# Products of a row with itself: pieces, places and rows on a 256-byte grid, and another order of the last waits

## Chip, cores and metric

The kernel runs on one core of one Trainium2 chip. The metric is the device time of one execution in microseconds. It was run three times before the change, and the median counts.

## What is computed

```python
# r_inputs: float32 (4096, 256)
d = inputs.shape[1]
dot = jnp.einsum('bi,bj->bij', inputs, inputs)
iu, ju = jnp.triu_indices(d)
return dot[:, iu, ju]          # float32 (4096, 32896)
```

Each of 4096 rows of 256 numbers becomes 32896 numbers: all products of two of its elements, with the second index not below the first. The 256 runs of an output row, one for each first index i, have the lengths 256, 255, ... 1. The input has 4.19 MB and the output 538.97 MB.

## The kernel before

**Tiling.** Partition p of 128 holds 32 input rows, all of them in `xt`, which stays on the chip for the whole run. Two rows at a time (`REPEAT`) are worked on together, so one round has 512 numbers a partition. There are 16 rounds, two to a pass (`PASS` of 6 pieces is two rounds of `PIECES` = 3). A round's output row of 32896 columns is cut into three pieces by `even_borders`, in steps of `UNIT` = 32 columns: 10944, 10976 and 10976 columns wide.

**Buffers.** There are two output places `o0` and `o1` (`PLACES`), each with two rows of `slot` = 10976 columns a partition; piece p goes to place p % 2. A place holds 87808 bytes a partition, its rows lie 43904 bytes apart. In the order of allocation the tiles are `xt`, `xv` (a copy of the round's input for VectorE and GpSimd), `xa` (the same for ScalarE, used at the start alone), and then the places; `xp`, in PSUM, is a further copy that VectorE reads. In the built program `xt` starts at byte 16512 of a partition, `xv` at 49280, `xa` at 51360, `o0` at 53408 and `o1` at 141216.

**Engines.** Each piece's runs are divided over engines. VectorE (L220) multiplies the row `xv` by a number from `xp` that is repeated along the run, with two neighbouring runs in one instruction where that is possible; GpSimd (L272) does the same from `xv` alone. The division in the loop gives GpSimd about 19.4 us of work by a cost formula and VectorE the rest. The first two pieces (`AHEAD`) come before the loop: for them ScalarE (L244) works beside VectorE in GpSimd's place, and the first piece leaves in five parts (`FIRST`) so that stores start early. ScalarE first copies its input to `xa` (L239).

**Order.** SyncE issues every DMA: three loads of the input (L327), which take 128 x 512, 3584 and 4096 numbers, and then one store for each piece or part (L298). A store waits for `v_done` and for `a_done` or `g_done`, and its landing adds 16 to `free0` or `free1`. Before it writes a place, VectorE waits for that place's landing and tells GpSimd by `go`. A pass of the loop (L310) makes pieces 2 to 5 of one pass and then 0 and 1 of the next. `take` (L164) is the helper that waits for a semaphore and takes the count off.

**The end.** After the loop SyncE passes six waits by `take`: `free0`, `free1`, then `x_read`, then the three `loaded`. Then all engines meet and the program ends.

One store row, 43904 bytes of one partition, is one DMA packet; each of the 16 DMA engines has 16 of the 256 rows of a store.

Of the kernel before, what the change touches and what calls it, by code (L numbers as in the profile page):

```python
# [8 lines left out]
F32 = mybir.dt.float32  # L9
AF = mybir.ActivationFunctionType  # L10
ALU = mybir.AluOpType

P = 128
UNIT = 32
REPEAT = 2
PIECES = 3
PLACES = 2
SETS = 2
PASS = 6
# [7 lines left out]
def even_borders(lo: int, hi: int, pieces: int) -> list[int]:  # L27
    units = (hi - lo) // UNIT
    return [lo + units * c // pieces * UNIT for c in range(pieces)] + [hi]

# [83 lines left out]
def kernel(  # L114
# [15 lines left out]
    nc = tc.nc  # L130
    n, d = x.shape
    width = out.shape[1]
    each, groups = REPEAT * d, n // (P * REPEAT)
    rounds = PASS // PIECES
    passes = groups // rounds
    assert n % (P * REPEAT) == 0 and width == d * (d + 1) // 2 and width % UNIT == 0
    assert PASS % PLACES == 0 and AHEAD == PLACES and PASS % PIECES == groups % rounds == 0
    borders = even_borders(0, width, PIECES)
    spans = list(zip(borders, borders[1:]))
    slot = max(b - a for a, b in spans)  # L140
# [2 lines left out]
    x_out = out.rearrange("(p h q r) c -> h q p r c", p=P, q=rounds, r=REPEAT)  # L143

    pool = ctx.enter_context(tc.tile_pool(name="all", bufs=1))
    xt = pool.tile([P, passes, rounds * each], F32, name="x")

    xv = pool.tile([P, each + 1], F32, name="xv")
    xa = pool.tile([P, each], F32, name="xa")

    xp = ctx.enter_context(tc.tile_pool(name="psum", bufs=1, space=bass.MemoryType.PSUM)).tile([P, each], F32, name="xp")
    places = [pool.tile([P, REPEAT, slot], F32, name=f"o{k}") for k in range(PLACES)]
    ctx.enter_context(tc.tile_critical())  # L153

    def semaphore(name: str):
        return ctx.enter_context(nc.semaphore(name))

    free = [semaphore(f"free{k}") for k in range(PLACES)]
    head, v_done, a_done, go = (semaphore(s) for s in ("head", "v_done", "a_done", "go"))
# [3 lines left out]
    def take(engine, sem, value: int):  # L163
        engine.wait_ge(sem, value).then_inc(sem, -value)  # L164

    v_own, a_own, g_own = (semaphore(s) for s in ("v_own", "a_own", "g_own"))
    g_done, x_read = semaphore("g_done"), semaphore("x_read")

    def x_of(h, q: int) -> bass.AP:
        return xt[:, bass.ds(h, 1), q * each : (q + 1) * each].rearrange("p o d -> p (o d)")  # L170

    def blocks(p: int, ahead: bool):

        lo, hi = spans[p % PIECES]
        cuts = [lo, *(FIRST if ahead and p == 0 else []), hi]
        for a, b in zip(cuts, cuts[1:]):
            block = runs(d, a, b)
            if ahead:
                k = split(block)
                yield a - lo, b - lo, block[:k], block[k:], lo  # L180
            else:
                k = next(k for k in range(len(block)) if gpsimd_time(block[k:]) <= BUDGET * 1e3)
                yield a - lo, b - lo, block[k:], block[:k], lo

    uses = PASS // PLACES

    def use(p: int) -> int:
        return (p - AHEAD) % PASS // PLACES + 1  # L190

    def vector(h, pieces: range, ahead: bool, done: int = 0) -> int:
        for p in pieces:
            place = places[p % PLACES]
            if p % PIECES == 0:
                if not ahead:
                    take(nc.vector, x_read, 1)
                for to in (xv[:, :each], xp):
                    ins = nc.vector.tensor_copy(to, x_of(h, p // PIECES))  # L199
                    if done:  # L200
# [35 lines left out]

    def scalar(pieces: range):

        nc.scalar.activation(xa, x_of(0, 0), AF.Copy).then_inc(a_own, 1)  # L239
        take(nc.scalar, a_own, 1)  # L240
        for p in pieces:
            for _, _, block, _, lo in blocks(p, True):
                todo = [
                    nc.scalar.activation(  # L244
                        places[p][:, r, at - lo : at - lo + length],
                        xa[:, r * d + j : r * d + j + length],
                        AF.Copy,
                        scale=xa[:, r * d + i : r * d + i + 1],
                    )
                    for i, j, at, length in block  # L250
                    for r in range(REPEAT)
                ]
                if todo:
                    todo[-1].then_inc(a_done, 1)
                else:
                    nc.scalar.sem_inc(a_done, 1)
# [45 lines left out]
    def all_pieces(engine, pieces_of):  # L302
        done = pieces_of(0, range(AHEAD), True)
        if engine is nc.vector:
            nc.vector.sem_inc(v_own, -done)
        if engine is not nc.sync:
            for sem in loaded[1:]:
                engine.wait_ge(sem, 16)
        kind = engine.engine
        with nc.Fori(  # L310
            0,
            passes,
            engines=OrderedEngineSet([kind]),
            head_slot={kind: 0} if engine is not nc.sync else {},
        ) as h:
            done = pieces_of(h, range(AHEAD, PASS), False)
            with engine.If(h < passes - 1):
                nxt = nc.s_assert_within(h + 1, 0, passes - 1)
                if engine is nc.vector:
                    nc.vector.sem_inc(v_own, -vector(nxt, range(AHEAD), False, done))  # L320
                else:
                    pieces_of(nxt, range(AHEAD), False)
        if engine is nc.vector:
            nc.vector.sem_inc(v_own, -done)
# [7 lines left out]
    take(nc.tensor, head, 16 * (len(FIRST) + 1))  # L332
    nc.tensor.sem_inc(free[0], 16)
    scalar(range(AHEAD))
    for engine, pieces_of in ((nc.vector, vector), (nc.gpsimd, gpsimd), (nc.sync, sync)):
        all_pieces(engine, pieces_of)
    for k in range(PLACES):
        take(nc.sync, free[k], 16 * uses)
    take(nc.sync, x_read, 1)
    for sem in loaded:  # L340
        take(nc.sync, sem, 16)


# [25 lines left out]
```

## Time and profile before

| what | value |
|---|---|
| median of 3 runs | 1270.35 us (1270.26 to 1270.4) |
| the profiled execution, given by its span alone | 1268.8 us |
| DVE busy | 794.1 us, 63% |
| POOL busy | 767.8 us, 61% |
| ACT busy | 29.9 us, 2% |
| queue 1 of the DMA | 99.5% of 16 engines |
| store of 10976 columns | 10976 KB, x32, 32.1 us from issue to landing (median) |
| store of 10944 columns | 10944 KB, x15, 33.6 us |

The span runs from the first to the last instruction of the program in the profile; the timed runs are 1.55 us above it, and the profile gives no other time for its execution. DVE is VectorE, ACT ScalarE, POOL GpSimd, SP SyncE; a small q behind a name stands for the engine's instruction queue. The time from issue to landing counts the time behind other stores in the same queue.

### The profile page before, as it was taken

What the parts mean: (1) busy time and instruction counts of PE and PEld (TensorE: products, weight loads), DVE (VectorE), ACT (ScalarE), POOL (GpSimd) and SP (SyncE); (2) the same over time, 40 slices, a digit from 0 to 9 for tenths busy, and PEclk for the clock granted to TensorE, in tenths of its full rate; (3) what the DMA queues carried; (4) which work ended last, traced back from release to release, by engine and by line L of the source; (5) the groups of instructions that cost most, each with busy time, mean ns of one, the idle gap of its engine ahead of it and who ended that gap; (6) DMA issues with size and microseconds to landing.
All of it is one profiled execution on the core that took longest, in us unless ns stands there. A gap on an engine that the chain in (4) does not pass through costs nothing. (4 is left out here: it accounts for less than half of the span.)

```text
span 1268.8 us, 3000 instructions
## 1 busy us (share of the span) xinstructions
DVE 794.1 (63%) x1197; ACT 29.9 (2%) x80; POOL 767.8 (61%) x1032
## 2 busy tenths in 40 slices
DVE  8756856567466674766648665486655866468560
ACT  9000000000000000000000000000000000000000
POOL 0467674676647765577556765567656675576750
DMA  9999999999999999999999999999999999999997
GB/s 379 438 437 425 439 431 433 434 428 433 431 435 429 437 426 438 426 437 424 439 425 439 427 436 429 435 430 433 430 433 428 435 421 441 421 442 421 438 425 336
DMA packets 14583, 543.22 MB, mean 428 GB/s; under 512 B 880, under 2 KB 880, under 8 KB 1520
## 3 DMA queue, kind: packets, MB, share of 16 engines
q1 hardware_dynamic: 14576, 543.17, 99.5%
q14 instruction: 7, 0.06, 0.0%
HBM read 4.19 MB, written 538.97 MB: 428 GB/s over the span
## 5 line engine op out<-in xcount | busy, mean ns | idle before, releaser
L272 POOL TENSOR_TENSOR o<-xv 128x292 f32<-128x292 f32 (+60 forms) x1028 | 767.6, 787 | 461.8 <-DVEq L207 322.1
L220 DVE TENSOR_TENSOR o<-xv,xp 128x512 f32<-128x512 f32 (+61 forms) x1164 | 776.1, 746 | 429.4 <-DMA out_dram<-o 303.8
L244 ACT ACTIVATE o<-xa 128x253 f32<-128x253 f32 (+38 forms) x78 | 27.9, 454 | 0.2 <-ACTq L164 0.2
L199 DVE COPY xv<-x 128x512 f32 (+1 forms) x16 | 6.8, 427 | 10.0 <-DVEq L164 7.2
L199 DVE COPY xp<-x 128x512 f32 (+1 forms) x16 | 11.1, 695 | 0.6
L239 ACT ACT_TABLE_LOAD x1 | 1.3, 1283 | 0.9 <-SPq L153 0.9
L328 DVE MEMSET xv<- 128x1 f32 x1 | 0.1, 59 | 1.0 <-SPq L153 1.0
L239 ACT ACTIVATE xa<-x 128x512 f32<-128x512 f32 x1 | 0.6, 631 | 1.7 <-DMA x<-in_r_inputs_dram 1.7
L356 POOL MEMSET const-float32-0.0<- 128x1 f32 x1 | 0.1, 98 | 0.2 <-issue 0.2
L356 POOL MEMSET const-bfloat16-1.0<- 128x1 bf16 x1 | 0.1, 101 | 0.0
L356 POOL MEMSET const-uint8-127<- 128x1 uint8 x1 | 0.1, 101 | 0.0
L356 POOL MEMSET const-float32-1.0<- 128x1 f32 x1 | 0.1, 98 | 0.0
## 6 DMA issues: line engine op xcount, KB each, us to landing
out_dram<-o SPq DMA_DIRECT2D x32, 10976.0 KB, 32.1
out_dram<-o SPq DMA_DIRECT2D x15, 10944.0 KB, 33.6
out_dram<-o SPq DMA_DIRECT2D x1, 4544.0 KB, 19.4
out_dram<-o SPq DMA_DIRECT2D x1, 2816.0 KB, 15.1
x<-in_r_inputs_dram SPq DMA_DIRECT2D x1, 2048.0 KB, 12.4
out_dram<-o SPq DMA_DIRECT2D x1, 2048.0 KB, 12.6
x<-in_r_inputs_dram SPq DMA_DIRECT2D x1, 1792.0 KB, 7.1
out_dram<-o SPq DMA_DIRECT2D x1, 1024.0 KB, 9.7
```

The lines of the kernel that those rows point to most:

```text
L199: ins = nc.vector.tensor_copy(to, x_of(h, p // PIECES))
L220: ins = nc.vector.tensor_tensor(place[:, :, at : at + m * length], window(xv[:, j:], [[d, REPEAT], [1, m], [1, length]]), window(xp[:, i:] ...
L239: nc.scalar.activation(xa, x_of(0, 0), AF.Copy).then_inc(a_own, 1)
L244: nc.scalar.activation(places[p][:, r, at - lo : at - lo + length], xa[:, r * d + j : r * d + j + length], AF.Copy, scale=xa[:, r * d + i ...
L272: ins = nc.gpsimd.tensor_tensor(place[:, :, at : at + m * length], window(xv[:, j:], [[d, REPEAT], [1, m], [1, length]]), window(xv[:, i:] ...
L328: nc.vector.memset(xv[:, each:], 0.0)
L356: nc = _bacc.Bacc("TRN2", target_bir_lowering=False, num_devices=1)
```

## The change

`UNIT` becomes 64 columns, 256 bytes, and the borders of the pieces move to 0, 10944, 21888 and 32896; the pieces are 10944, 10944 and 11008 columns wide. A tile `edge` of 32 numbers, which nothing uses, comes first, then the places, then `xt` and `xv`. In the built program `o0` starts at byte 16640, `o1` at 104704, `xt` at 192768 and `xv` at 225536; all four are multiples of 256, and so is the distance of 44032 bytes between the rows of a place. ScalarE has no copy of its own: `xa` is now the first 512 numbers of `xt`, and the copy and its wait are gone. SyncE's last waits come in the order `x_read`, the three `loaded`, `free0`, `free1`.

```diff
-UNIT = 32
+UNIT = 64
 REPEAT = 2
 PIECES = 3
+EDGE = 32
 ...
     pool = ctx.enter_context(tc.tile_pool(name="all", bufs=1))
+    pool.tile([P, EDGE], F32, name="edge")
+    places = [pool.tile([P, REPEAT, slot], F32, name=f"o{k}") for k in range(PLACES)]
     xt = pool.tile([P, passes, rounds * each], F32, name="x")
-
     xv = pool.tile([P, each + 1], F32, name="xv")
-    xa = pool.tile([P, each], F32, name="xa")
 
     xp = ctx.enter_context(tc.tile_pool(name="psum", bufs=1, space=bass.MemoryType.PSUM)).tile([P, each], F32, name="xp")
-    places = [pool.tile([P, REPEAT, slot], F32, name=f"o{k}") for k in range(PLACES)]
 ...
-    v_own, a_own, g_own = (semaphore(s) for s in ("v_own", "a_own", "g_own"))
+    v_own, g_own = (semaphore(s) for s in ("v_own", "g_own"))
 ...
     def scalar(pieces: range):
 
-        nc.scalar.activation(xa, x_of(0, 0), AF.Copy).then_inc(a_own, 1)
-        take(nc.scalar, a_own, 1)
+        xa = xt[:, 0, :each]
 ...
-    for k in range(PLACES):
-        take(nc.sync, free[k], 16 * uses)
     take(nc.sync, x_read, 1)
     for sem in loaded:
         take(nc.sync, sem, 16)
+    for k in range(PLACES):
+        take(nc.sync, free[k], 16 * uses)
```

## The prediction

> **What bounds the kernel now.** I read the DMA rows of the page first, because the output is 539 MB and the engines are idle a third of the time.
>
> ```profile
> DVE 794.1 (63%) x1197; ACT 29.9 (2%) x80; POOL 767.8 (61%) x1032
> ...
> DMA  9999999999999999999999999999999999999997
> ...
> q1 hardware_dynamic: 14576, 543.17, 99.5%
> ...
> HBM read 4.19 MB, written 538.97 MB: 428 GB/s over the span
> ```
>
> No compute engine passes 63%, and the DMA row is full in every slice but the last. Queue 1, which carries the three loads and all stores, fills 99.5% of the span. The second view is the waits, to see whether the DMA waits for the engines or they for it.
>
> ```profile
> POOL o L272 <- DVEq L207: 322.1, 32, 43.1
> DVE o L220 <- DMA out_dram<-o: 303.8, 31, 12.3
> ...
> DVE o L220 <- DVEq L164: 119.2, 14, 12.4
> ```
>
> VectorE waits for stores to land and so to free a place (L164 is the waiting helper, and DVEq L207 the wait that releases GpSimd). The stores never wait long for VectorE. The third view, busy time in stretches, gives the pace of the stores.
>
> ```profile
> 66.00:92.00 26.00, 13.72 (x14) 0.00 (x0) 17.94 (x12) 1.00 1.00 434
> ...
> 470.00:548.00 78.00, 49.15 (x75) 0.00 (x0) 49.97 (x66) 1.00 1.00 432
> ...
> 1184.00:1210.00 26.00, 14.63 (x19) 0.00 (x0) 17.70 (x16) 1.00 1.00 431
> 1236.50:1262.40 25.90, 0.00 (x0) 0.00 (x0) 0.00 (x0) 1.00 0.96 414
> 1240.00:1266.80 26.80, 0.00 (x0) 0.00 (x0) 0.00 (x0) 1.00 0.80 346
> 1266.80:1268.80 2.00, 0.00 (x0) 0.00 (x0) 0.00 (x0) 1.00 0.00 0
> ```
>
> The columns are the length, the three engines, the clock, the DMA share and GB/s. The pace is 431 to 434 GB/s, whatever the engines do beside it. The last 2.0 us hold no transfer. From 1262.4 to 1266.8 only part of the DMA engines still works: the packet records show one engine that ends 4.3 us after the median of the others. That engine never runs dry, and it sets the end. The time is therefore: start of the stream, plus the packets of one DMA engine, plus the 2.0 us after them.
>
> [...]
>
> **The change, part by part.**
>
> *Addresses of the stores.* In the program built from the kernel before, places start at byte 160 past a multiple of 256, and with a row of 43904 bytes their second row starts at 32 past. [...] One packet is one row of one piece. A DMA engine carries 16 of the 256 rows of each of 47 whole pieces and of the 5 parts of the first: 832 packets. [...]
>
> Does the trace charge it? The packet records say no, in three ways. First, in the head the median store packet of 2048, 4096, 8192, 11264 and 18176 bytes took 84, 159, 309, 422 and 676 ns: a line of 36.7 ns a KB (1000 bytes) that leaves 8.8 ns at zero length. Records of one DMA engine overlap by 3.5 ns, so a packet really loses about 5.3 ns[...]. Second, the loads, whose source rows do start at multiples of 256, lie on the same line: 84 ns for 2048 bytes and 535 for 14336. Third, [...]in each head part nearly all packets have one and the same duration (309 from the 1st to the 75th percentile and beyond, at 8192 bytes). I take 0.5 ns a packet, 832 x 0.5 = 0.4 us[...].
>
> *Borders in the output.* Rows of the third piece started at 128 past a multiple of 256, those of the first at 0. Once the stream has settled, three pieces in a row took 26.03, 26.02 and 25.94 us (second, third, first; semaphore to semaphore). The first has 43776 bytes a row, not 43904; scaled by that it would be 26.02. So a border off the grid costs 0.00 to 0.01 us a piece, over the 32 second and third pieces at most 0.3 us. I take zero, as bytes in all are unchanged.
>
> [...]In the loop the median packet of 43904 bytes took 1627 ns and the mean is some 1630, where the line gives 1620.5. These 7 to 10 ns are not the offsets, which the head had too without them: the first whole pieces were at 1622, and they rise once the DMA engines drift apart. I price the change on them at zero, and keep plus or minus 3 ns for the range (2.5 us).
>
> *ScalarE's copy.* One ACTIVATE of 631 ns and its wait go, and ScalarE starts at about 3.9 us instead of 4.71.
>
> ```profile
> 3.88 0.63 ACT L239 ACTIVATE xa<-x 128x512 f32<-128x512 f32 x1 [1.69 <-DMA x<-in_r_inputs_dram]
> 4.71 27.95 ACT L244 ACTIVATE o<-xa 128x253 f32<-128x253 f32 x78 [0.20 <-ACTq L164]
> 5.08 32.03 DVE L220 TENSOR_TENSOR o<-xv,xp 128x512 f32<-128x512 f32 x45
> 6.59 31.10 SPq L298 DMA_DIRECT2D out_dram<-o  x6
> ```
>
> ScalarE ended at 32.7 us and VectorE at 37.1, and the issue at 37.3 followed VectorE. The first parts are covered twice: the loads held the queue until 14 us and each of the five parts was issued over 5 us before the queue came to it. Worth 0. If that cover were gone it would be worth 0.8 us at most.
>
> *Pieces of 10944, 10944, 11008 columns* (before 10944, 10976, 10976). The built program shortens one GpSimd and one VectorE instruction of the second piece by 64 elements and lengthens one VectorE instruction of the third by 64: 64 x 1.07 ns (from 1222 ns for 1024 elements and 1020 for 836) = 0.07 us, beside 19.92 us for that piece (last group of the chain). It is covered on the DMA engine that sets the end, which has 4.3 us of work left when the last store is issued; on the others only some 0.2 us is left by then, and they do not count. The last store is 32 KB longer, 0.08 us, but the bytes of a DMA engine are the same in all: 0.
>
> *SyncE's last waits.* The last packet ends at 1266.80, its semaphore rises at 1267.28, and SyncE then passes five waits, for place 1, x_read and three loads, at 1267.295, .362, .428, .496 and .562. After the change only that for place 1 stands behind the landing; the others had long been met. Four times 0.067 = **0.27 us** less, on the path, as everything after waits for SyncE.
>
> Sum: 0.27 + 0.4 = 0.7 us less. The span of 1268.8 becomes 1268.1; the median of the runs stands 1.55 above that span, and I take that distance to stay: 1270.35 - 0.7 = **1269.6**. [...]
>
> **The rivals.**
>
> [...]
>
> *Slower: rows in step.* All places, rows and borders now fall on the same phase of 256 bytes, and if the DMA engines get more into each other's way, packets lengthen. The place is the loop; the trace shows such growth, from 1622.7 ns mean for the second whole store to 1630 later. Another 4 ns is 832 x 4 = 3.3 us: 1273.0. It decides from 2.54 / 832 = 3.1 ns. Against it: each packet keeps its length and its DMA engine.
>
> *Engines become the bound.* If xv and the places at new addresses slowed VectorE, the third piece's 19.92 us would have to grow by 4.3 us (22%) before the latest DMA engine runs dry. Nothing speaks for it: the same instructions run on the same operands. Past that point every place that waits for this piece adds the excess.
>
> *The change does nothing but the tail:* 1270.1, inside the first case.
>
> **How the numbers follow.** A measurement of this kernel can tell about 0.2%, 2.54 us: faster is below 1267.8, slower above 1272.9. First case with the tail alone: 0.70. Offsets at full price or more: 0.21. Rows in step or slower engines: 0.09; of these about 0.02 stays below 1272.9. So faster 0.21, same 0.72, slower 0.07. The range runs from 1266.9[...] to 1271.2, which leaves out the slower case and the part of the faster one that adds the drift, and takes in a drift that worsens by 1 to 2 ns.
>
> **What would show it.** Right: a pace of 432 to 433 GB/s in the same stretches, median packets near 1622 ns (43776 bytes) and 1632 (44032), one wait of SyncE after the last landing and the end some 1.75 us after the last packet; ScalarE's first ACTIVATE at 3.9 and no earlier first landing. Wrong: packets on or below the head's line (1616 and 1625 ns) and 434 GB/s or more, which is the offsets; packets 4 ns longer, which is the rows in step; DMA slices under 9 inside the loop, which is the engines.

## The result, and the profile after

| | median | range | runs |
|---|---|---|---|
| before | 1270.36 us | 1270.23 to 1270.63 | 16 |
| after | 1267.88 us | 1267.78 to 1268.03 | 16 |

The ratio of after to before is 0.998, with a 95% interval of 0.9974 to 0.9987. The kernel is 2.48 us faster, 0.2%. The profiled span fell by 2.7 us, from 1268.8 to 1266.1.

These are the lines of the page of after that answer to those of before.

```profile
DVE 795.2 (63%) x1197; ACT 29.2 (2%) x79; POOL 766.1 (61%) x1032
...
DMA  9999999999999999999999999999999999999997
...
q1 hardware_dynamic: 14576, 543.17, 99.4%
...
HBM read 4.19 MB, written 538.97 MB: 429 GB/s over the span
```

Nothing changed its role: the DMA is full and the engines have time. The waits of after say the same; VectorE waits for places as long as it did (302.0 us now, 303.8 before).

```profile
POOL o L271 <- DVEq L207: 322.5, 32, 43.0
DVE o L220 <- DMA out_dram<-o: 302.0, 31, 12.3
```

Busy time in stretches of after (length, three engines, clock, DMA share, GB/s):

```profile
66.00:92.00 26.00, 13.72 (x14) 0.00 (x0) 17.93 (x12) 1.00 1.01 437
470.00:548.00 78.00, 49.36 (x75) 0.00 (x0) 49.98 (x67) 1.00 1.01 435
1184.00:1210.00 26.00, 14.63 (x19) 0.00 (x0) 17.59 (x16) 1.00 1.00 431
1236.50:1262.40 25.90, 0.00 (x0) 0.00 (x0) 0.00 (x0) 1.00 0.89 384
...
1260.50:1264.50 4.00, 0.00 (x0) 0.00 (x0) 0.00 (x0) 1.00 0.05 22
1264.50:1266.10 1.60, 0.00 (x0) 0.00 (x0) 0.00 (x0) 1.00 0.00 0
```

The pace in the middle rose from 432 to 435 GB/s, and yet the last row but one is what counts: over the last 4.0 us a share of 0.05 of 16 DMA engines moves data, which is about one of them. The stretch before the end shows the same in the kernel before:

```profile
1262.60:1266.80 4.20, 0.00 (x0) 0.00 (x0) 0.00 (x0) 1.00 0.05 21
```

So the other DMA engines became faster (median packet in the loop 1622 ns for 43776 bytes and 1627 for 43904 before, 1618 for 43776 and 1627 for 44032 after), and then wait at the places, which are free only when all 16 have landed, for the one that is late. It sets the time as before. The packet records do not name the DMA engines; the late one is followed by the last of a store's 16 semaphore packets, one from each DMA engine (880 packets under 512 bytes for 55 transfers). What it needs for a piece (from one such packet to the next, mean of the pieces of the loop) is the key to all that follows. The row lengths are in brackets.

| kernel | first piece, us | second | third |
|---|---|---|---|
| before | 25.95 (43776 B) | 26.24 (43904) | 26.06 (43904) |
| after | 25.93 (43776) | 26.11 (43776) | 26.07 (44032) |

The second piece lost 128 bytes a row and 0.13 us; the third gained 128 bytes a row and next to nothing. Each comes once in 16 rounds: 16 x 0.13 = 2.1 us, and the shorter end of the program gives 0.3 (experiment 6).

### The profile page after: what moved, and what is told of

Its sections match the earlier page's. It is cut to its first block, busy times and chain, and to the rows that moved or that the text cites. A ratio compares the mean times of both kernels' runs of the same rounds, so it can differ in the third digit from the quotient of the medians.

```text
span 1266.1 us, 2998 instructions
## 1 busy us (share of the span) xinstructions
DVE 795.2 (63%) x1197; ACT 29.2 (2%) x79; POOL 766.1 (61%) x1032
## 5 line engine op out<-in xcount | busy, mean ns | idle before, releaser
L220 DVE TENSOR_TENSOR o<-xv,xp 128x512 f32<-128x512 f32 (+61 forms) x1164 | 777.1, 748 | 426.3 <-DMA out_dram<-o 302.0
L243 ACT ACTIVATE o<-x 128x253 f32<-128x253 f32 (+38 forms) x78 | 28.0, 454 | 0.0
```

The lines of the kernel that those rows point to most:

```text
L220: ins = nc.vector.tensor_tensor(place[:, :, at : at + m * length], window(xv[:, j:], [[d, REPEAT], [1, m], [1, length]]), window(xp[:, i:] ...
L243: nc.scalar.activation(places[p][:, r, at - lo : at - lo + length], xa[:, r * d + j : r * d + j + length], AF.Copy, scale=xa[:, r * d + i ...
```

## The experiments

The times of the kernel before in these comparisons were 1270.38, 1270.38 and 1270.39 us.

**1. Borders back.** Only the borders in the output leave the grid again; the rows in the places stay on it.

```diff
-UNIT = 64
+UNIT = 32
-    slot = max(b - a for a, b in spans)
+    slot = -(-max(b - a for a, b in spans) // 64) * 64
```

Theory G has every packet cost the same extra whose source row and output row stand at different distances from the 256-byte grid; theory B has the borders in the output alone count.

> The changed kernel with the borders of the pieces back at 10944 and 21920 columns (steps of 32); places, rows and input stay on the 256-byte grid. [...] Theory G[...]: only the third piece's rows start at 128 past, a third of the packets lose what they lost before: 1268.6. Theory B (borders in the output are what counted): as before but for the tail, 1270.1, with the third piece's packets alone longer.

Measured: 1270.27 us (1270.13 to 1270.46), ratio to before 0.9999 [0.9991, 1.0008]. Nearly the whole gain is gone, so it came from the borders. The DMA engine that ends last needs 25.94, 26.24 and 26.06 us for the three pieces, which are the numbers of before; the longer piece is the second and not the third, as theory B had it. The page of this kernel shows the 2.4 us in the span, and its stretches a pace in the middle as high as that of after:

```profile
span 1268.5 us, 2998 instructions
```

```profile
470.00:548.00 78.00, 49.15 (x75) 0.00 (x0) 49.96 (x66) 1.00 1.01 435
```

In this run the packets of the other DMA engines hardly vary: the median in the loop is 1618 ns for 43776 bytes and 1622 for 43904, where before had 1622 and 1627. It brought no time.

**2 to 4. The places off the grid by 32, 128 and 224 bytes.** The borders stay on the grid.

```diff
-EDGE = 32
+EDGE = 40      # 64 and 88 in the other two
```

> The changed kernel with every tile 32 bytes further, so that all source rows start at 32 past a multiple of 256 and the output stays on the grid. [...] G: any offset costs the same, about as before less the tail: 1270.1. B: 1267.9.

> The same with 128 bytes. [...] G: 1270.1; if what counts is a grid of 64 bytes and not of 256, 1267.9. B: 1267.9.

> The same with 224 bytes. [...] G: 1270.1, also if the grid has 64 bytes. B: 1267.9.

Measured: 1267.66 (1267.48 to 1267.82), 1267.71 (1267.54 to 1267.93) and 1267.74 us (1267.56 to 1267.88), ratios 0.9979 [0.997, 0.9987] for each of the first two and 0.9979 [0.9971, 0.9987] for the third. 32, 128 and 224 bytes of distance cost the same: nothing that the time shows. The distance of the source rows from the grid does not set the time here, and theory G falls. The offsets are visible all the same. With each of the three distances the median packet in the loop is 1622 ns (43776 bytes) and 1632 (44032), where after has 1618 and 1627. Busy time in stretches of the kernel with 32 bytes:

```profile
470.00:548.00 78.00, 49.34 (x75) 0.00 (x0) 50.03 (x67) 1.00 1.00 431
...
1184.00:1210.00 26.00, 14.63 (x19) 0.00 (x0) 17.61 (x16) 1.00 1.00 431
...
1261.80:1264.30 2.50, 0.00 (x0) 0.00 (x0) 0.00 (x0) 1.00 0.04 18
```

The pace in the middle is back at 431 GB/s from 435, while the time is 0.2 us shorter than after. The last row tells why: the late DMA engine, which sets the end, is alone for some 2.5 us here and for 4.0 in after; it ends at 1264.3 in one and 1264.5 in the other. A faster mean pace was spent on waiting for it.

**5. Borders off by 32 bytes.** Both inner borders move by 8 columns.

```diff
-    borders = even_borders(0, width, PIECES)
+    borders = [0, 10952, 21896, width]
```

Theory W counts 256-byte blocks of the output: on the DMA engine that ends last, a row that starts or ends inside a block costs as much as one that fills it.

> The changed kernel with both inner borders 8 columns (32 bytes) further, at 10952 and 21896. Theory W[...]: a round's three rows of pieces touch 172 + 172 + 172 = 516 of them, against 514 in the changed kernel and 515 before. One more costs 9.4 ns a packet, x 16 packets x 16 rounds = 2.4 us, so two cost 4.8: 1272.7 us. [...] Rival, bytes alone: 1267.9.

Measured: 1272.72 us (1272.57 to 1272.9), ratio 1.0018 [1.0011, 1.0026], to the tenth what theory W said, and 4.8 us over after. On the DMA engine that ends last the first piece went from 25.93 to 26.07 us: 16 packets that are 32 bytes longer, 1.2 ns at the 36.7 ns for 1000 bytes of the head's packets, took 8.4 ns more each. The second, with rows of 43776 bytes as in after but across the grid, went from 26.11 to 26.27. The third, whose 44000 bytes touch 172 blocks like the 44032 of after, stayed within 0.02. The size of the block is not settled by this, and no record shows blocks as such; the count fits the times. With blocks of 128 bytes before and after would count the same (1028 a round), and they differ by 2.4 us; but blocks of 512 bytes fit as well as 256: an output row is 257 of them, so that successive rows start on and half a block off their grid, and the means of a round are 258.5 in after, 259 in before and 259.5 here, the same steps of 256 bytes. The page:

```profile
span 1271.2 us, 2996 instructions
```

**6. The tail alone,** on the kernel before.

```diff
-    for k in range(PLACES):
-        take(nc.sync, free[k], 16 * uses)
     take(nc.sync, x_read, 1)
     for sem in loaded:
         take(nc.sync, sem, 16)
+    for k in range(PLACES):
+        take(nc.sync, free[k], 16 * uses)
```

> The kernel before with SyncE's last waits in the new order and nothing else. By the profile before, four waits of 0.067 us leave the end: 0.27 us less, 1270.1. The run with the borders set back stood only 0.11 us under the kernel before though it has the new tail; if the timed runs see less of the end than the profile does, 1270.25.

Measured: 1270.06 us (1269.98 to 1270.29), 0.32 less than before; the ratio, 0.9998 [0.9989, 1.0006], does not tell it from no change by itself. The medians agree with the four waits of 0.067 us.

**7. The tail and ScalarE's part,** on the kernel before.

```diff
-        nc.scalar.activation(xa, x_of(0, 0), AF.Copy).then_inc(a_own, 1)
-        take(nc.scalar, a_own, 1)
+        xa = xt[:, 0, :each]
```

> The kernel before with the new order of the last waits and without ScalarE's copy (it reads the input tile; every address stays where it was). The prediction said that the copy is covered by VectorE, which ends later in both first pieces: as the last waits alone, 1270.1. Rival: the sum of the parts so far (tail 0.3, borders 2.4) is 0.2 us more than the whole change brought; if ScalarE's part, whose table load now comes after the wait for data, is what costs it, 1270.3; if not, the addresses of the places cost it.

Measured: 1270.12 us (1269.96 to 1270.24), ratio 0.9998 [0.999, 1.0006]: with the tail alone it was 1270.06, so ScalarE's part is worth nothing in either direction.

**8. More instructions.** ScalarE gets work that nobody waits for.

```diff
+    with nc.Fori(0, EXTRA // 40, engines=OrderedEngineSet([nc.scalar.engine])):
+        for _ in range(40):
+            nc.scalar.activation(spare, xt[:, 0, : spare.shape[1]], AF.Copy).then_inc(a_own, 1)
+            take(nc.scalar, a_own, 1)
```

> The changed kernel; ScalarE, idle in the loop, executes 2000 extra activations of 64 elements on a tile of its own, each with a semaphore wait. Theory I (the one DMA engine that ends last loses time for each instruction that engines execute, 3.5 ns or so: its pieces are longest while VectorE and GpSimd run their 77 shortest instructions): 2000 to 4000 more instructions x 3.5 ns = 7 to 14 us: 1275 to 1282, if it happens without a profiler too; if it is the profiler's doing, the profiled span alone grows and the timed runs stay at 1267.9. Rival (that engine is slow for its own reasons): span and time as the changed kernel.

Measured: 1282.24 us (1282.11 to 1282.33), ratio 1.0093 [1.0078, 1.0109], 14.4 us over after. The page and the stretches:

```profile
span 1280.4 us, 7100 instructions
...
DVE 795.1 (62%) x1197; ACT 541.6 (42%) x2079; POOL 767.1 (60%) x1032
...
q14 instruction: 7, 0.06, 0.0%
```

```profile
470.00:548.00 78.00, 47.88 (x74) 52.08 (x204) 48.57 (x66) 1.00 0.97 420
1274.70:1278.80 4.10, 0.00 (x0) 0.00 (x0) 0.00 (x0) 1.00 0.05 21
```

The stores, VectorE and GpSimd do what they did. There are 4102 more instructions, and 14.4 us / 4102 = 3.5 ns for each. The last line is the queue that the profile names instruction; after has 7 packets there too. Again one DMA engine is alone at the end, and the share of 0.97 in the middle is that of the others waiting for it.

**9. Fewer instructions.** In the loop, VectorE and GpSimd execute one product of each piece and leave out the others; all stores stay. Two memsets, not shown, fill the end of the places.

```diff
-                order = interleave(block)
+                order = interleave(block) if ahead else interleave(block)[:1]
 ...
-            order = interleave(block)
+            order = interleave(block)[:1]
```

> The changed kernel with all but one VectorE and one GpSimd product of each piece left out in the loop; all stores and waits stay, so the stream is the same without the engines' work. I: the last DMA engine loses its lag of 4 us at the end; span about 1262 and time 1264 (or span alone, if the profiler does it). Rival (own reasons): lag and time as in the changed kernel, 1267.9. If the engines' work slows all DMA engines: below 1262.

Measured: 1261.34 us (1261.18 to 1261.45), ratio 0.9928 [0.9914, 0.9941], 6.5 us under after. The page:

```profile
span 1259.7 us, 945 instructions
...
DVE 78.0 (6%) x126; ACT 29.2 (2%) x79; POOL 57.3 (5%) x50
```

That is 2053 instructions less, 3.2 ns for each. The DMA engine that ends last now needs 25.83, 25.83 and 25.98 us (medians of the three pieces), which is what the other fifteen need; the second piece, the longest in after, no longer stands out. Over 99% of the loop's packets take 1618 or 1627 ns. The late engine's lag, 1.5 us, dates from the start and does not grow: two packets of queue q14, 8192 bytes each, run at 41.8 and 47.3 us for 0.31 and 0.32 us, and the store packets right behind them take 1976 and 2100 ns in place of 1618. That adds up to 1.5 us, so the late DMA engine is most likely the one that carries these two. So theory I holds: most of the rest of the lag of after comes with executed instructions. Engine time does not explain it: this kernel lacks 1426 us of engine time and gained 6.5 us, while ScalarE's 512 us more cost 14.4. Semaphore updates explain it as well as instructions do, for the traces record 3554 in after, 7554 in experiment 8 and 1683 here, which makes 3.6 and 3.5 ns for each; no run changes the one without the other.

**10. Columns taken from the sixteenth DMA engine.**

```diff
+                main = hi - lo - (192 if p == PASS - 1 else 0)
 ...
+                if p == PASS - 1:
+                    for a, b in ((0, 120), (120, P)):
+                        nc.sync.dma_start(to[a:b, :, main:], place[a:b, :, lo + main : hi]).then_inc(sem, 16)
```

The 27.2 GB/s of one DMA engine is 1000 bytes in the 36.7 ns of the head's packets.

> The changed kernel, but the last 192 columns of the sixth piece of each pass leave in two stores of their own, of partitions 0 to 119 and 120 to 127. If 120 partitions are spread over the first 15 DMA engines and 8 over the first 8, the sixteenth carries none of these columns: 8 x 16 x 768 bytes at 27.2 GB/s, 3.6 us less for it, and 0.06 us a pass more for the first 8. Theory L (one DMA engine sets the end, and it is the sixteenth): [...]1264.7. Rival, the late one is one of the first 8: 1268.7. Rival, one in between, or the end is not set by one DMA engine: 1268.0 to 1268.3.

Measured: 1269.64 us (1269.51 to 1269.85), ratio 0.9994 [0.9986, 1.0003], 1.8 us more than after. None of the three forecasts was met, but the run tells something of where the late DMA engine is. The DMA view of this kernel:

```profile
DMA packets 16816, 543.23 MB, mean 428 GB/s; under 512 B 1064, under 2 KB 3112, under 8 KB 3752
...
out_dram<-o SPq DMA_DIRECT2D x8, 180.0 KB
...
out_dram<-o SPq DMA_DIRECT2D x8, 12.0 KB
```

The packets under 512 bytes are the semaphore increments, one a store and DMA engine: 1064 - 880 = 184 = 8 x (15 + 8), so the two small stores did use 15 and 8 DMA engines. In the last pass the late one closes all three stores, at 1265.32, 1265.86 and 1265.93 us: it takes part in both small ones, and therefore is one of the eight that carry the smallest store, not the one that was left out. It got more to do instead of less; why 1.8 us and not the 0.8 of that rival, no run shows.

## Why the prediction was right or wrong, by its steps

The time lay in the range and the sum had the right sign, but it was 0.7 us where 2.48 were measured. That is just inside the 2.54 us called no change. That the time lay in the range was in part luck: its lower end had been drawn for dearer source offsets, which no run shows, and the time came from elsewhere. The term of the borders failed, the 0.4 us of the offsets did not come, and the tail was right.

**Borders in the output: the step that failed.** I took zero and at most 0.3 us; the runs show 2.4 (1270.27 with the borders back, 1267.88 without). The inference was to scale the pace of three pieces by their bytes. The paces I used, 26.03, 26.02 and 25.94, were means over the sixteen DMA engines, although I had found before that one of them sets the end. On the fifteen others bytes are what counts (1618 and 1622 ns for 43776 and 43904 bytes in experiment 1), and the scaling is right. On the late one the loop's rows cost, in sum, what whole 256-byte blocks of the output would: the records of before had 26.06 us for a third piece of 43904 bytes and after has 26.07 for 44032. A round's three rows touch 171 + 172 + 172 = 515 before and 514 after. One less is 256 bytes, 9.4 ns at the 36.7 ns for 1000 bytes of the head's packets, in 16 packets of 16 rounds: an estimate of 2.4 us. The same count put two more at 4.8 us for experiment 5, and 4.8 were measured.

**Offsets of the source: 0.4 us less was forecast.** The 0.5 ns a packet under it was my estimate, which no packet record shows. The reading that the trace does not charge them holds, for the time: 32, 128 and 224 bytes gave 1267.66 to 1267.74. No gain came of it. By the medians the places on the grid even cost 0.1 to 0.2 us: 1267.66 to 1267.74 against 1267.88, and 1270.06 (tail alone) against 1270.27 (borders back). The ranges of these runs overlap, and the intervals of the ratios, some 0.1% to either side, do not tell so little from nothing.

**The packets of the loop.** I said that the 7 to 10 ns in the loop are not the offsets, since the head had these too. This was wrong: with the places on the grid the loop's packets fell to 1618 and 1627 ns, within 3 ns of the head's line, and in experiments 2 to 4 they rose again. The head is no measure of it; there the same offsets show nothing (median packets of 84, 159, 309, 422 and 676 ns before and after). It brought no time because the DMA engine that ends last did not take part in the gain. So the sign that the prediction named for the offsets, 434 GB/s or more with packets near the head's line, came true while the time came from the borders.

**The tail.** 0.27 us forecast; in the profile the time from the last landing to the end fell from 1.48 to 1.21 us, and the medians show 0.32 with the tail alone. Right.

**ScalarE.** Nothing, as forecast, and the cover I named held. One detail was wrong: its first product does not start at 3.9 us but later than before, because the table load, which before stood ahead of the wait for data (at 0.92 us), now follows it.

```profile
3.85 1.28 ACT L243 ACT_TABLE_LOAD   x1 [3.85 <-DMA x<-in_r_inputs_dram]
...
4.96 31.97 DVE L220 TENSOR_TENSOR o<-xv,xp 128x512 f32<-128x512 f32 x45
5.14 27.95 ACT L243 ACTIVATE o<-x 128x253 f32<-128x253 f32 x78
```

ScalarE ends at 33.1 us and VectorE at 36.9, so VectorE still covers it.

**The other widths.** No engine became the bound; the third piece's VectorE work grew from 19.92 to 19.99 us, the 0.07 us forecast, and nothing of it shows in the time.

**The rivals.** The case of dearer offsets, which the prediction gave 0.21, did not come: with the offsets back the time stayed at 1267.66 to 1267.74 (experiments 2 to 4). "Rows in step" went the other way: the packets became shorter and more even, not longer (43776 bytes at a median of 1618 ns against 1622, a mean of 1619.1 against 1624.1). That the one DMA engine is late by itself was in no rival; I took its lag as given and did not ask what makes it.

What stays open is why the count of blocks fits this DMA engine alone, and what each instruction takes from it. I thought that the two belong together: that a DMA engine which loses time to instructions has none left to make up for blocks that are only partly filled. The last store speaks against it: VectorE ends at 1235.1 us in the kernel before, and yet the late DMA engine needs 25.97 us for its rows of 43904 bytes, from 1240.8 to 1266.8. That is near the 25.99 of after for 44032 and above the 25.91 that bytes alone make, halfway between the 25.83 and 25.98 of experiment 9. Nor is it a charge on every row: ten of the 16 packets take 1622 ns, the length that bytes give, and the rest 5 to 19 ns more. The count of blocks gives the sum and not the single packet.

What takes an instruction's 3.2 to 3.5 ns is not shown. It is not the packets of queue q14, of which there are 7 in after and in experiment 8, 5 in experiment 9, and none between 145 us and the end of the stores. Nor is it settled whether the profiling has a part in it. The timed runs moved with the profiled ones (14.4 and 14.3 us in experiment 8), but each timed run on record has its span and clock beside it, so no run here shows an execution without any recording.

## What to carry to other kernels

When a stream of transfers sets the time, find the DMA engine that ends last and read its pieces, not the mean rate: here the mean in the middle rose by 3 GB/s where nothing was gained (experiment 1), and stayed at 431 in experiment 2, whose time is that of after. Where the time is as close to the DMA as here, try cuts of the output rows at multiples of 256 bytes, which were worth 2.4 us of 1270 here, and count the blocks that each cut adds. An engine with idle time may not be free either: 2000 tiny activations that nobody waited for, each with its semaphore wait, cost 14 us as measured here.

## What the runs showed of the hardware

One DMA engine, among the eight that a store of 8 partitions uses (it closes the last of these at 1265.93 us in experiment 10), ends 3.2 to 3.5 ns later for each instruction that the engines execute, waits included (945, 2998 and 7100 instructions: 1261.34, 1267.88 and 1282.24 us), or 3.5 to 3.6 ns for each semaphore update; that this holds without recording is not shown. With ScalarE's 2000 activations and their waits beside it a full stream took 14.4 us longer (experiment 8); the share of the 16 DMA engines in the middle was 0.97 there and 1.01 in after. On the same DMA engine the third piece's rows of 43904 bytes, which start off the grid of the output, cost as much as those of 44032 (26.06 and 26.07 us for 16 of them). Places at 32, 128 or 224 bytes off the grid are not slower than on it (1267.66, 1267.71 and 1267.74 us against 1267.88).
